# Layer 2 attention of a four-layer graph network: half of the middle graphs form their exponentials as [column, row], with squares on ScalarE

## The chip, the cores and the metric

The kernel runs on one core of a Trainium2 chip. The metric is the device time of one execution in microseconds (us), the median of three runs. PE is TensorE, PEld its weight load, DVE is VectorE, ACT is ScalarE, POOL is GpSimd and SP is SyncE.

## What is computed

32 graphs of 512 nodes with 128 features (x is 32 x 512 x 128, f32) share one adjacency matrix of 512 x 512. Four layers run one after the other, each as x = x + layer(relu(layernorm(x))). Cut to what matters here:

```
layer 0: h = x @ Wo; e[k] from pairs of u1 = h@a1, u2 = h@a2 (leaky, 0.1), masked by adj
         softmax over axis 1;  out = att @ h + x @ Ws
layer 1: h = x @ Wp + bp; scores[i,j] = leaky(src[i] + dst[j], 0.2), masked by A
         attn = softmax(scores, axis=-1) * A;  g = relu(layernorm(attn @ h) * gg + gb)
         z = relu(layernorm(((1+eps) g + A @ g) @ W1 + b1) * mg + mb);  out = relu(z @ W2 + b2 + g)
layer 2: h = x @ W; e[i,j] = leaky(f1[i] + f2[j], 0.2), -9e15 where adj[i,j] <= 0
         out = elu(softmax(e, axis=2) @ h + bias)
layer 3: out = (A3's diagonal) * (x @ W0) + (A3 without it) @ (x @ W1) + bias
```

## The kernel before, in words

A graph lies in SBUF as `xs[:, b]`, [128 partitions, 4 chunks, 128 features]: node 128c + p is partition p of chunk c. Nothing loops on the chip: the program is written out operation by operation, for every graph and layer.

**The order.** Every operation goes through `op(engine, length, emit, reads, writes)` (L130) into the `Plan`. Each layer of each graph is one chain; chains are put in order by `order` (L1320 to L1327), with `LAGS` (a layer's delay in graphs) and `GAPS` (the time between chains), stretched by `RAMP` for the first `AHEAD` graphs. `Plan.run` (L158) is a list scheduler that works before the chip does: among the operations whose inputs are there it takes the one that could begin first by the lengths given (`SLACK` apart counts as equal, then the one with the earlier turn), and emits it. The order on each engine is thus fixed and each engine works through its queue in that order. At most `WINDOW` = 20 chains are open. Buffers come from `Room`s: eight PSUM `banks`, eight `scores` tiles of [128, 4, 128] f32, six `by_act`, five `by_dve` and so on; an operation that needs a new tile waits in the plan until its room has one free. `op.port` marks operations of DVE and POOL that the plan does not let overlap. Where PE would sit idle for over `PAUSE` in the plan, `idle_products` (L331) puts in transposes whose result nobody reads. `PREPARED` and `FILLED` give the turns of the set-up of later layers' weights and masks, which runs beside the first graphs. `EARLY` says for how many graphs layer 0 normalizes on ACT rather than POOL.

**Pieces.** `preln` (L530) normalizes a graph: `variances` (L503) takes bn_stats and bn_aggr on DVE, four of each; `inv_dev` (L518) takes the power -1/2 on POOL; the normalized `xn` is transposed on PE (`turn_op`, L416, four transposes into one bank) and passed through Relu on ACT as `hT`. `project_scored` (L586) multiplies by a weight extended by two columns, so `h` has 130 columns: 128 features, the source score (column P) and the target score (column P + 1). `repeated(col)` (L604) writes a column, broadcast over 128, through four transposes, so that a bank `prow` holds the 512 values as a row in every partition.

**Attention in layers 1 and 2** is `attend` (L610). Rows i lie on partitions: for each of the four row chunks DVE adds `prow` (target scores) to the mask `bias` and takes the row's maximum (L622); two small operations make `nmax`, the negative maximum after the leaky step (L633, L637). Then, one chunk after the other: Prelu on ACT with the source score as bias (L647), Exp on ACT with `nmax` as bias and the row's sum as accumulated output (L655), four transposes on PE (L661) into a bank, a copy out as `pT` (in layer 2 two chunks on ACT, two on DVE, L666 to L671; in layer 1 a multiplication by the adjacency on DVE, L664), and four matmuls with `pT` as the stationary operand and `h` as the moving one (L675). An f32 matmul is two MATMUL instructions in the profile, a transpose is one. Layer 2 (L942) then takes the reciprocal of the sums and one DVE multiplication `v1` (L955), adds the bias on POOL (L956) and forms the elu.

**Layer 1** after its attention: variances of `po` on DVE (L886) go with the sums into a power on POOL; later the variances of `zn` on DVE (L923) go through `inv_dev`. **Layer 0** scales `h` by two per-node factors on DVE, `hs` (L805) and `hs2` (L806), and takes a masked maximum against `biasT`, the first half of the columns of the transposed mask (L727).

The lines that follow are those of the kernel before, as in the profile.

Of the kernel before, what the change touches and what calls it, by code (L numbers as in the profile page):

```python
# [35 lines left out]
AX = mybir.AxisListType  # L36

P = 128
NEG = -9.0e15
LOWEST = -3.0e38  # L40
LN_EPS = 1e-5

# [20 lines left out]

RAMP = 4.1

PAUSE = 0.6

EARLY = 8

GAPS, LAGS = (5.3, 12.0, 6.7, 5.4), (0, 6, 12, 16)  # L70


class Room:
# [38 lines left out]
class Plan:  # L112
# [45 lines left out]
    def run(self):  # L158
# [17 lines left out]
        for _ in range(len(self.ops)):  # L176
            while oldest < len(normal) and not left[normal[oldest]]:
                oldest += 1
            best = None
            for engine, ops in ready.items():  # L180
                could = []
                for op in ops:
                    k = op.chain
                    beside = self.chains[k][1] is not None
                    if not beside and order[k] >= oldest + WINDOW:
                        continue
                    begin = max(idle[engine], op.ready)
# [24 lines left out]
            if op.engine is PE and idle[PE] and begin - idle[PE] > PAUSE:  # L212
                wanted = sum(s.tile is None and s.room is self.banks for s in op.slots)
                if sum(free <= idle[PE] for free in self.banks.free) > wanted:
                    self.idle_products(begin - idle[PE])
            ready[op.engine].remove(op)
            for s in op.slots:
                if s.tile is None:
                    s.room.free.remove(min(s.room.free))
                    s.tile = s.room.make(s.name)  # L220
            end = begin + op.length
            idle[op.engine] = end
            if op.port:
                piece = op.length / op.port
                held[op.engine] = [(begin + k * piece, begin + (k + 1) * piece - HOLD) for k in range(op.port)]
            done = end + DELAY[op.engine]
            if op.load:
                bus = max(done, bus) + op.load
                done = bus
            if op.transfers:  # L230
                lanes = lanes[op.transfers :] + [done] * op.transfers
            op.emit()
            traced = nc.cur_bb.bb.instructions
            while seen < len(traced):
                ins = traced[seen]
                seen += 1
                if ins.engine in last:
                    tc.add_manual_dep(
                        ins, last[ins.engine].name,
                        mybir.DependencyInfo(mybir.DependencyClass.NoSync, mybir.DependencyReason.DATA),  # L240
                        reason="the plan's order",
                    )
                last[ins.engine] = ins
            left[op.chain] -= 1
            for s in op.slots:
                s.users -= 1
                s.until = max(s.until, done)
# [10 lines left out]
def kernel(  # L258
# [143 lines left out]
    v_offT, v_adiag, v_adiag_rep = Value(), Value(), Value()  # L402
# [37 lines left out]
    load(lambda: wt_o.t[:, 0, :], l0_wo, [wt_o], 0.25)  # L440
    load(lambda: att, l0_att.rearrange("(t p) o -> p (t o)", p=P), [v_att])
    for ib in range(C):
        load(lambda ib=ib: bias[:, ib, :], adj[blk(ib), :], [v_adj[ib]], 1.0)
    load(lambda: wts[:, W_S, :], l0_ws, [v_wts[W_S]], 0.25)
    for b in range(1, AHEAD):
        load_x(b)
# [37 lines left out]

    def mask_first():
        for jb in range(C):
            nc.vector.tensor_scalar(biasT[:, jb, :], adjT[:, jb, 0:N2], 0.0, NEG, ALU.is_le, ALU.mult)

    op(DVE, 0.85, mask_first, v_adjT[0:H], [v_biasT], port=C)

# [24 lines left out]
        dve(1.1, emit, reads, [mv])  # L515
        return mv

    def inv_dev(mv):  # L518
        rstd = Value()

        def emit():
            ve = small("ve")
            nc.gpsimd.tensor_scalar(ve, mv.own[:, :, 1], LN_EPS, 1.0, ALU.add, ALU.mult)
            rstd.own = small("rstd")
            nc.gpsimd.tensor_tensor(rstd.own, ve, mhalf, ALU.pow)  # L525

# [160 lines left out]
    def layer0(b):  # L687
# [31 lines left out]
        for hf in range(H):  # L719

            def emit_max(hf=hf):
# [3 lines left out]
                for k in range(2):  # L725
                    jb = 2 * hf + k
                    nc.vector.tensor_tensor_reduce(  # L727
                        wide(y[hf].t)[:, k * N2 : k * N2 + N2], node[:, hf, :], biasT[:, jb, :], 1.0, LOWEST,
                        ALU.add, ALU.max, rmax.own[:, jb : jb + 1],
                    )  # L730

# [74 lines left out]
        op(DVE, 0.6, lambda: nc.vector.tensor_mul(hs2.t, h[0].t[:, :, 0:P], per_chunk(rs2.own)), [rs2, *h], [hs2], port=1)  # L806

        hi, lo = [], []
        for hf in range(H):
# [51 lines left out]
    def layer1(b):  # L861
# [18 lines left out]

        def emit_ve():
            ve.own = small("ve1")
            nc.vector.tensor_add(ve.own, q.own, mv.own[:, :, 1])
# [39 lines left out]
        rz = inv_dev(variances(lambda c: zn.t[:, c, :], [zn]))  # L923

        def emit_zn():
            for c in range(C):
# [12 lines left out]
           [res], [v_x[b]], port=1)  # L939


    def layer2(b):  # L942
        hT, _ = preln(b, POOL)
        h = project_scored(hT, w2_ext, [v_w2])
        po, ssum = attend(h, lambda: h[0].t[:, :, P], h, h, None, None)
        v1 = value(by_dve, "v1")

# [5 lines left out]

        dve(0.1, emit_rs, ssum, [rs])
        dve(0.6, lambda: nc.vector.tensor_mul(v1.t, po[0].t, per_chunk(rs.own)), [*po, rs], [v1])  # L955
        op(POOL, 1.25, lambda: nc.gpsimd.tensor_add(v1.t, v1.t, row_of(B_L2)), [v_rows], [v1], port=1)  # L956


# [36 lines left out]
    def prepare():  # L995
# [24 lines left out]
        for ib in range(C):  # L1020
            dve(0.31, lambda ib=ib: nc.vector.tensor_scalar(
                bias[:, ib, :], bias[:, ib, :], 0.0, NEG, ALU.is_le, ALU.mult), [], [v_adj[ib], v_bias], port=1)
        score_weights(lambda: wt_p.t[:, 0, :], wt_p, a1[:, 0:2], v_a1, w1_ext[:, P:P2], v_w1)
        score_weights(lambda: wt_l2.t[:, 0, :], wt_l2, a2, v_a2, w2_ext[:, P:P2], v_w2)
        copy_op(DVE, 0.15, lambda: w2_ext[:, 0:P], lambda: wt_l2.t[:, 0, :], [wt_l2], [v_w2])
# [336 lines left out]
```

## Time and profile before

| | us |
|---|---|
| median of 3 runs | 1061.43 (1060.64 to 1062.57) |
| the profiled execution, its own time | 1063.87 |
| its span | 1062.1 |
| PE busy | 1041.7 (98%), 8475 instructions |
| PEld busy | 966.0 (91%) |
| DVE busy | 868.5 (82%) |
| ACT busy | 780.5 (73%) |
| POOL busy | 776.2 (73%) |

The span goes from the first to the last instruction that the profiler recorded on the core. The busy time of an engine is the union of its instructions, so where one begins before the one ahead of it has ended, the sum of the durations is larger. On PE above all: a matmul of 128 columns has a mean duration of 275 ns, and its successor starts long before it has ended. What an instruction takes away from the others is therefore read from start to start on the timeline, not from its duration. The granted clock is that of TensorE as a share of full speed.

### The profile page before, as it was taken

How to read it: one execution, taken by the hardware profiler on the slowest of the kernel's cores; microseconds unless marked ns; L12 is line 12 of the kernel's file. 1: busy time of each engine (PE TensorE's matmuls, PEld its weight loads, DVE VectorE, ACT ScalarE, POOL GpSimd, SP SyncE). 2: the span in 40 equal slices, each digit the busy share in tenths (PEclk: the TensorE clock that was granted, in tenths of full speed). 3: DMA queues.
4: the chain of work that ended last, by engine and by line, in shares of the span. 5: the costliest groups of instructions: out<-in, count | busy, mean ns of one | idle time of the engine just before them, and what ended most of it. 6: DMA issues, size and time to landing. Idle time of an engine off the chain costs nothing.

```text
span 1062.1 us, 25166 instructions
## 1 busy us (share of the span) xinstructions
PE 1041.7 (98%) x8475; PEld 966.0 (91%) x8475; DVE 868.5 (82%) x3694; ACT 780.5 (73%) x2024; POOL 776.2 (73%) x1140
## 2 busy tenths in 40 slices
PE   7899999999999999999999999999999999999998
PEld 7789789989999999999999999999899999999997
DVE  7799999989988878888888888888888877766752
ACT  6768897789877777777877777787777777767751
POOL 4489577778787777787778778777877666576772
PEclk9899999999999999999999999999999999999999
DMA  6400000000010000000000000000000000000001
GB/s 181 96 12 2 1 2 21 2 12 11 2 31 2 21 21 21 22 21 12 2 12 11 12 12 12 11 2 11 12 11 11 11 11 11 11 22 11 22 24 37
DMA packets 56912, 20.49 MB, mean 19 GB/s; under 512 B 21584, under 2 KB 56272, under 8 KB 56784
## 3 DMA queue, kind: packets, MB, share of 16 engines
q1 hardware_dynamic: 56784, 18.90, 7.2%
q8 instruction: 67, 1.10, 0.5%
q14 instruction: 61, 0.50, 0.2%
HBM read 10.43 MB, written 8.39 MB: 18 GB/s over the span
## 4 chain that ended last, share of the span: by engine, by line
PE 88%; DVE 4%; POOL 3%; DMA 1%; SPq 1%; issue 1%; ACT 1%; POOLq 0%; DVEq 0%; ACTq 0%
PE po L675 20%; PE pt L421 16%; PE po L984 10%; PE pg L911 10%; PE proj L595 7%; PE po L837 5%; PE prow L421 3%; PE p L581 3%; PE pz L581 3%; PE px L581 3%; PE po L980 3%; PE po L842 2%; PE po L834 1%; PE po L847 1%; POOL xn L560 1%
## 5 line engine op out<-in xcount | busy, mean ns | idle before, releaser
L675 PE MATMUL po<-h,pT 128*128 128x128 f32 x2048 | 242.8, 275 | 0.8 <-DVE pT L664 0.8
L675 PEld LDWEIGHTS po<-h,pT 128*128 128x128 f32 x2048 | 236.4, 192 | 5.8 <-issue 4.1
L560 POOL TENSOR_SCALAR xn<-xs,shift,rstd 128x128 f32<-128x128 f32 x480 | 213.1, 459 | 2.8 <-DVE top L633 0.9
L655 ACT ACTIVATE y<-y,nmax 128x512 f32<-128x512 f32 x256 | 181.7, 714 | 5.3 <-DVE nmax L637 4.6
L525 POOL TENSOR_TENSOR rstd<-ve,mhalf 128x4 f32<-128x4 f32 x160 | 170.9, 1068 | 13.3
L622 DVE CUSTOM_DVE_ANT_0 y<-prow,bias 128x512 f32<-128x512 f32 x256 | 162.8, 683 | 1.6 <-PE prow L421 1.6
L984 PE MATMUL po<-h,offT 128*128 128x128 f32 x1024 | 135.4, 275 | 0.0
L911 PE MATMUL pg<-adjTe,hg 128*128 128x512 f32 x256 | 131.0, 593 | 0.0
L421 PE MATMUL pt<-ident,y 128*128 128x128 f32 x1024 | 130.2, 274 | 0.7 <-ACT hl L819 0.7
L421 PEld LDWEIGHTS pt<-ident,y 128*128 128x128 f32 x1024 | 115.1, 141 | 13.8 <-issue 8.5
L984 PEld LDWEIGHTS po<-h,offT 128*128 128x128 f32 x1024 | 124.6, 192 | 0.0
L511 DVE BATCH_NORM_STATS2 st<-xs 128x6 f32<-128x128 f32 x512 | 109.8, 277 | 7.2 <-POOL xs L962 4.5
L595 PEld LDWEIGHTS proj<-w_ext,hT 128*128 128x128 f32 x768 | 96.8, 192 | 19.0 <-issue 9.6
L595 PE MATMUL proj<-w_ext,hT 128*128 128x130 f32 x768 | 102.9, 277 | 1.4 <-ACT hT L570 1.3
L647 ACT ACTIVATE y<-y,src 128x512 f32<-128x512 f32 x128 | 84.6, 714 | 20.8 <-DVE rmax L622 19.6
L962 POOL TENSOR_TENSOR xs<-xs,em 128x512 f32<-128x512 f32 x32 | 42.0, 1312 | 76.8 <-DVE em L961 63.8
L956 POOL TENSOR_TENSOR v<-v,rows 128x512 f32<-128x512 f32 x32 | 40.9, 1279 | 72.4 <-DVE v L955 72.4
L570 ACT ACTIVATE hT<-pt 128x512 f32<-128x512 f32 x128 | 73.5, 589 | 25.3 <-PE pt L421 14.0
L647 ACT ACTIVATE y<-y,h 128x512 f32<-128x512 f32 x128 | 84.7, 714 | 7.9 <-DVE rmax L622 7.7
L664 DVE TENSOR_TENSOR pT<-pt,adjT 128x512 f32<-128x512 f32 x128 | 82.6, 681 | 5.7 <-PE pt L421 5.6
L421 PE MATMUL pt<-ident,xn 128*128 128x128 f32 x512 | 77.8, 274 | 1.5 <-POOL xn L560 1.3
L412 ACT COPY h<-proj 128x260 f32<-128x260 f32 x192 | 66.1, 371 | 13.4 <-PE proj L595 12.4
(204 smaller groups left out, 2302.3 us busy)
## 6 DMA issues: line engine op xcount, KB each, us to landing
xs<-in_x_dram SPq DMA_DIRECT2D x32, 256.0 KB, 4.0
out_dram<-yo SPq DMA_DIRECT2D x32, 256.0 KB, 2.3
u<-h SPq DMA_DIRECT2D x128, 0.5 KB, 1.8
bias<-in_adj_dram SPq DMA_DIRECT2D x4, 256.0 KB, 4.4
wts<-in_L_gnn_W_dram SPq DMA_DIRECT2D x3, 64.0 KB, 4.2
rows<-in_L_gnn_bias_dram SPq DMA_DIRECT2D x2, 64.0 KB, 3.7
wt_o<-L_gnn_others_weight_dram SPq DMA_DIRECT2D x1, 64.0 KB, 2.5
wts<-n_L_gnn_self_weight_dram SPq DMA_DIRECT2D x1, 64.0 KB, 4.5
```

The source lines that it names most:

```text
L421: nc.tensor.transpose(dst(k), src(k), ident)
L511: nc.vector.bn_stats(st[:, c, :], src(c))
L525: nc.gpsimd.tensor_tensor(rstd.own, ve, mhalf, ALU.pow)
L560: nc.gpsimd.tensor_scalar(xn.t[:, c, :], src[:, c, :], shift.own[:, c : c + 1], rstd.own[:, c : c + 1], ALU.add, ALU.mult,)
L581: nc.tensor.matmul(pt.t[:, c, :], lhsT=column(hT, c), rhs=w, start=True, stop=True)
L595: nc.tensor.matmul(p[:, c, :], lhsT=column(hT, 2 * k + c), rhs=w_ext, start=True, stop=True)
L622: nc.vector.tensor_tensor_reduce(wide(y[ib].t), wide(prow.t), bias[:, ib, :], 1.0, LOWEST, ALU.add, ALU.max, rmax.own[:, ib : ib + 1],)
L647: nc.scalar.activation(yw, yw, AF.Prelu, alpha=0.2, bias=src()[:, ib : ib + 1])
L655: nc.scalar.activation(yw, yw, AF.Exp, bias=nmax.own[:, ib : ib + 1], accum_out=ssum[0].own[:, ib : ib + 1])
L675: nc.tensor.matmul(po[ib].t[:, ib, :], lhsT=pT.t[:, jb, :], rhs=h[0].t[:, jb, 0:P], start=(jb == 0), stop=(jb == C - 1),)
L911: nc.tensor.matmul(wide(pg.t), lhsT=hg.t[:, nb, :], rhs=adjTe[:, nb, :], start=(nb == 0), stop=(nb == C - 1))
L984: nc.tensor.matmul(po[ib].t[:, ib, :], lhsT=offT[:, jb, blk(ib)], rhs=h1.t[:, jb, :], start=False, stop=(jb == C - 1),)
```

## The change

`TURNED = (3, 27, 2)` picks the graphs 3, 5, 7 ... 25. In those, layer 2's attention no longer has rows on partitions when it takes the exponentials. The row maxima are found as before, into a `junk` tile. Then `p_src` and `p_max` bring the source scores and the negative maxima into two PSUM banks as rows; `r_max` is a copy of the second in SBUF. For each chunk jb of columns, DVE adds the target score (per partition), the source scores and the transposed mask; ACT takes Prelu; DVE or POOL (in turns) adds the maxima; ACT takes Exp. The result is already [column, row], and is the stationary operand of the matmuls with no transpose and no copy. The sums of the rows come from a column of ones, which is written over the source scores in `h`, so the moving operand has 129 columns. Each two chunks of rows share a bank, and are divided by their sums on DVE.

In the same graphs, the two variances of layer 1 (of `po` and `zn`) are taken on ACT as squares with an accumulated sum, and `hs2` of layer 0 is formed on ACT. `biasT` now holds all 512 columns, in bf16, and NEG is -2^53 for it. `shift`, `mv` and `rstd` get a pool with 14 buffers (8 before). The lengths and turns that the plan uses are changed.

```diff
-NEG = -9.0e15
+NEG = -(2.0**53)
+PAIRED = 1.4
-STRETCH = 3.7
-PREPARED, FILLED = (35.0, 1.2), (109.0, 1.5)
-RAMP = 4.1
+STRETCH = 3.4
+PREPARED, FILLED = (43.0, 1.2), (106.0, 1.9)
+RAMP = 3.4
-EARLY = 8
-GAPS, LAGS = (5.3, 12.0, 6.7, 5.4), (0, 6, 12, 16)
+EARLY = 10
+GAPS, LAGS = (5.0, 11.3, 6.3, 5.1), (0, 5, 11, 15)
+TURNED = (3, 27, 2)
+def is_turned(b):
+    return TURNED[0] <= b < TURNED[1] and b % TURNED[2] != 0
...
-            done = end + DELAY[op.engine]
+            done = end + (PAIRED if op.transfers > 1 else DELAY[op.engine])
...
+    sm_norm = ctx.enter_context(tc.tile_pool(name="sm_norm", bufs=14))
     def small(name, shape=(P, C)):
-        return sm.tile(list(shape), F32, name=name, tag=name)
+        pool = sm_norm if name in ("shift", "mv", "rstd") else sm
+        return pool.tile(list(shape), F32, name=name, tag=name)
...
-    biasT = const("biasT", (P, C, N2))
+    biasT = const("biasT", (P, C, N), BF16)
...
-        load(lambda: xs[:, b], x[b].rearrange("(c p) f -> p c f", p=P), [v_x[b]], 1.0)
+        load(lambda: xs[:, b], x[b].rearrange("(c p) f -> p c f", p=P), [v_x[b]], 1.35)
...
+    def squares(src, reads):
+        sq = Value()
+        def emit():
+            sq.own = small("sq")
+            for c in range(C):
+                nc.scalar.activation(sq_out, src(c), AF.Square, accum_out=sq.own[:, c : c + 1])
+        op(ACT, 1.55, emit, reads, [sq])
+        return sq
...
-        op(SP, 1.8, emit_pair, h, [u], transfers=4)
+        op(SP, 2.6, emit_pair, h, [u], transfers=4)
...
+        def emit_hs2():
+            for c in range(C):
+                nc.scalar.mul(hs2.t[:, c, :], h[0].t[:, c, 0:P], rs2.own[:, c : c + 1])
+        if is_turned(b):
+            op(ACT, 1.17, emit_hs2, [rs2, *h], [hs2])
+        else:
+            op(DVE, 0.6, lambda: nc.vector.tensor_mul(hs2.t, h[0].t[:, :, 0:P], per_chunk(rs2.own)), [rs2, *h], [hs2], port=1)
...
-        mv = variances(lambda c: po[0].t[:, c, :], po)
+        mv = (squares if is_turned(b) else variances)(lambda c: po[0].t[:, c, :], po)
...
+        if is_turned(b):
+            rz = inv_dev(squares(lambda c: zn.t[:, c, :], [zn]), lambda sq: sq.own, 1.0 / P)
+        else:
+            rz = inv_dev(variances(lambda c: zn.t[:, c, :], [zn]))
...
+    def weighed_turned(h):
+        prow = repeated(lambda k: h[0].t[:, k, P + 1 : P2], h)
+        junk = parts(scores, "junk", C)
...
+                nc.vector.tensor_tensor_reduce(
+                    wide(junk[ib].t), wide(prow.t), bias[:, ib, :], 1.0, LOWEST, ALU.add, ALU.max,
+                    rmax.own[:, ib : ib + 1],
+                )
...
+        p_src = repeated(lambda k: h[0].t[:, k, P : P + 1], h)
+        p_max = repeated(lambda k: nmax.own[:, k : k + 1], [nmax])
+        r_max = value(by_act, "r_max")
+        copy_op(ACT, 0.49, lambda: wide(r_max.t), lambda: wide(p_max.t), [p_max], [r_max])
+        y = [value(scores, "y") for _ in range(C)]
+        for jb in range(C):
+            op(DVE, 0.67, lambda jb=jb: nc.vector.scalar_tensor_tensor(
+                wide(y[jb].t), wide(p_src.t), h[0].t[:, jb, P + 1 : P2], biasT[:, jb, :], ALU.add, ALU.add),
+               [p_src, v_biasT, v_biasT2, *h], [y[jb]])
+            op(ACT, 0.61, lambda jb=jb: nc.scalar.activation(wide(y[jb].t), wide(y[jb].t), AF.Prelu, alpha=0.2), [], [y[jb]])
+            if jb % 2:
+                op(DVE, 0.61, lambda jb=jb: nc.vector.tensor_add(
+                    wide(y[jb].t), wide(y[jb].t), wide(p_max.t)), [p_max], [y[jb]])
+            else:
+                op(POOL, 1.25, lambda jb=jb: nc.gpsimd.tensor_add(
+                    wide(y[jb].t), wide(y[jb].t), wide(r_max.t)), [r_max], [y[jb]], port=1)
+            op(ACT, 0.61, lambda jb=jb: nc.scalar.activation(wide(y[jb].t), wide(y[jb].t), AF.Exp), [], [y[jb]])
+        ones = Value(h[0].slot)
+        op(POOL, 0.15, lambda: nc.gpsimd.memset(h[0].t[:, :, P : P + 1], 1.0), [neg, p_src], [*h, ones])
+        po = [value(banks, "po") for _ in range(H)]
...
+                    nc.tensor.matmul(
+                        sums(ib // 2)[:, ib % 2, 0 : P + 1], lhsT=y[jb].t[:, ib, :], rhs=h[0].t[:, jb, 0 : P + 1],
+                        start=(jb == 0), stop=(jb == C - 1),
+                    )
+            op(PE, 0.9, emit_po, [*y, ones], [po[ib // 2]])
...
+            dve(0.1, emit_rs, [po[k], *rs[0:k]], [rs[k]])
+            dve(0.35, lambda k=k: nc.vector.tensor_mul(
+                v1.t[:, 2 * k : 2 * k + 2, :], sums(k)[:, :, 0:P],
+                rs[0].own[:, 2 * k : 2 * k + 2].rearrange("p (c o) -> p c o", o=1).to_broadcast([P, 2, P]),
+            ), [po[k], rs[k]], [v1])
+        return v1
...
+        v1 = (weighed_turned if is_turned(b) else weighed)(h)
...
+        for jb in range(C):
+            dve(0.2, lambda jb=jb: nc.vector.tensor_scalar(
+                biasT[:, jb, N2:], adjT[:, jb, N2:], 0.0, NEG, ALU.is_le, ALU.mult), v_adjT, [v_biasT2], port=1)
```

More of the change, by code (lines that the diff above doesn't have):

```diff
@@ L401 @@
     v_bias, v_w1, v_w2, v_wz, v_row_p, v_row_1, v_score_p, v_adjTe, v_rows, v_mlp = (Value() for _ in range(10))
-    v_offT, v_adiag, v_adiag_rep = Value(), Value(), Value()
+    v_offT, v_adiag, v_adiag_rep, v_biasT2 = (Value() for _ in range(4))
     def load(dst, src, writes, size=0.0):
@@ L486, in mask_first @@
         for jb in range(C):
-            nc.vector.tensor_scalar(biasT[:, jb, :], adjT[:, jb, 0:N2], 0.0, NEG, ALU.is_le, ALU.mult)
+            nc.vector.tensor_scalar(biasT[:, jb, 0:N2], adjT[:, jb, 0:N2], 0.0, NEG, ALU.is_le, ALU.mult)
     op(DVE, 0.85, mask_first, v_adjT[0:H], [v_biasT], port=C)
@@ L516, in variances, with inv_dev @@
         return mv
-    def inv_dev(mv):
+    sq_out = const("sq_out", (P, P))
+    def squares(src, reads):
[6 more added lines that the diff above has]
+        return sq
+    def inv_dev(mv, of=lambda mv: mv.own[:, :, 1], share=1.0):
         rstd = Value()
@@ L522, in emit @@
             ve = small("ve")
-            nc.gpsimd.tensor_scalar(ve, mv.own[:, :, 1], LN_EPS, 1.0, ALU.add, ALU.mult)
+            nc.gpsimd.tensor_scalar(ve, of(mv), share, LN_EPS, ALU.mult, ALU.add)
             rstd.own = small("rstd")
@@ L882, in emit_ve @@
             ve.own = small("ve1")
-            nc.vector.tensor_add(ve.own, q.own, mv.own[:, :, 1])
+            if is_turned(b):
+                nc.vector.scalar_tensor_tensor(ve.own, mv.own, 1.0 / P, q.own, ALU.mult, ALU.add)
+            else:
+                nc.vector.tensor_add(ve.own, q.own, mv.own[:, :, 1])
         dve(0.08, emit_q, ssum, [q], port=1)
-        mv = variances(lambda c: po[0].t[:, c, :], po)
+        mv = (squares if is_turned(b) else variances)(lambda c: po[0].t[:, c, :], po)
         dve(0.08, emit_ve, [q, mv], [ve], port=1)
@@ L955, in layer2, with emit_top, emit_neg, emit_nmax @@
         dve(0.6, lambda: nc.vector.tensor_mul(v1.t, po[0].t, per_chunk(rs.own)), [*po, rs], [v1])
+        return v1
+    def weighed_turned(h):
+        prow = repeated(lambda k: h[0].t[:, k, P + 1 : P2], h)
+        junk = parts(scores, "junk", C)
+        rmax = Value()
+        top = [Value() for _ in range(C)]
+        for ib in range(C):
+            def emit_top(ib=ib):
+                if ib == 0:
+                    rmax.own = small("rmax")
+                nc.vector.tensor_tensor_reduce(
+                    wide(junk[ib].t), wide(prow.t), bias[:, ib, :], 1.0, LOWEST, ALU.add, ALU.max,
+                    rmax.own[:, ib : ib + 1],
+                )
+            op(DVE, 0.61, emit_top, [prow, v_bias], [junk[ib], top[ib]])
+        neg, nmax = Value(), Value()
+        def emit_neg():
+            neg.own = small("top")
+            nc.vector.scalar_tensor_tensor(neg.own, rmax.own, -1.0, h[0].t[:, :, P], ALU.mult, ALU.subtract)
+        def emit_nmax():
+            nmax.own = small("nmax")
+            nc.vector.scalar_tensor_tensor(nmax.own, neg.own, 0.2, neg.own, ALU.mult, ALU.min)
+        dve(0.08, emit_neg, [*top, *h], [neg], port=1)
+        dve(0.08, emit_nmax, [neg], [nmax], port=1)
+        p_src = repeated(lambda k: h[0].t[:, k, P : P + 1], h)
[11 more added lines that the diff above has]
+                    wide(y[jb].t), wide(y[jb].t), wide(p_max.t)), [p_max], [y[jb]])
+            else:
+                op(POOL, 1.25, lambda jb=jb: nc.gpsimd.tensor_add(
[4 more added lines that the diff above has]
+        po = [value(banks, "po") for _ in range(H)]
+        def sums(k):
+            return po[k].t.rearrange("p (c t) f -> p c (t f)", c=2)
+        for ib in range(C):
+            def emit_po(ib=ib):
+                for jb in range(C):
[4 more added lines that the diff above has]
+            op(PE, 0.9, emit_po, [*y, ones], [po[ib // 2]])
+        v1 = value(by_dve, "v1")
+        rs = [Value() for _ in range(H)]
+        for k in range(H):
+            def emit_rs(k=k):
+                if k == 0:
+                    rs[0].own = small("rs")
+                nc.vector.reciprocal(rs[0].own[:, 2 * k : 2 * k + 2], sums(k)[:, :, P])
+            dve(0.1, emit_rs, [po[k], *rs[0:k]], [rs[k]])
[3 more added lines that the diff above has]
+            ), [po[k], rs[k]], [v1])
+        return v1
```

15 lines of the change are left out of this document (8 added, 7 removed).

## The prediction, on record before the run

> **What bounds the kernel now.** I read the stage windows first: busy time of each engine in each stretch, with the granted clock.
>
> ```profile
> 0.00:50.00 50.00, 39.48 (x306) 36.12 (x307) 37.97 (x235) 34.71 (x106) 21.67 (x40) 0.97 0.57 142
> 50.00:100.00 50.00, 48.43 (x395) 46.29 (x394) 45.36 (x225) 37.74 (x115) 46.19 (x76) 0.96 0.07 12
> 100.00:150.00 50.00, 47.96 (x358) 42.22 (x357) 49.12 (x219) 38.54 (x107) 33.42 (x42) 1.00 0.02 2
> ...
> 200.00:300.00 100.00, 100.00 (x805) 91.58 (x805) 92.88 (x407) 84.19 (x226) 79.84 (x117) 1.00 0.03 7
> ...
> 500.00:600.00 100.00, 100.00 (x823) 92.91 (x823) 82.05 (x354) 72.64 (x190) 79.14 (x118) 1.00 0.05 12
> ```
>
> Columns after the stretch's length: PE, PEld, DVE, ACT, POOL, clock, DMA share, GB/s. From 200 us on PE is busy all the time at full clock, while DVE, ACT and POOL have 7 to 28% left. Before 150 us PE misses 14.1 us (50 - 39.48, 50 - 48.43, 50 - 47.96), and the windows of the tile "idle" add 131 filler products there (90 and 41).
>
> A busy PE need not be a full PE, so next I read the starts on PE's timeline:
>
> ```profile
> 501.82 1.91 PE L421 MATMUL pt<-ident,y 128*128 128x128 f32 x16
> 503.57 0.60 PE L421 MATMUL pt<-ident,zn 128*128 128x128 f32 x4
> 504.01 1.06 PE L595 MATMUL proj<-w_ext,hT 128*128 128x130 f32 x8
> 504.90 1.02 PE L911 MATMUL pg<-adjTe,hg 128*128 128x512 f32 x2
> ...
> 507.59 3.74 PE L675 MATMUL po<-h,pT 128*128 128x128 f32 x32
> 511.16 0.60 PE L421 MATMUL prow<-ident,h 128*128 128x128 f32 x4
> ```
>
> Start to start, 16 transposes take 1.75 us (0.109 each), 8 matmuls of 130 columns 0.89 (0.111 each), 32 of 128 columns 3.57 (507.59 to 511.16, 0.112 each); two of 512 columns take 0.86 (the next piece, not shown, starts at 505.76). An f32 matmul in the code is two of these instructions, a transpose one. Now the work of one graph, counts divided by 32: 64 transposes x 0.109 = 7.0; 176 matmul instructions of 128 or 130 columns x 0.112 = 19.7; 8 of 512 x 0.43 = 3.4; 8 of 256 x 0.14 = 1.1 (4 in 0.56 us at 506.12). Sum 31.2 us. The chain that ended last shows the same burst of 32 `po` at 507.75, 538.89, 570.13 and 601.27: a graph every 31.1 us. Work equals period, so **PE's throughput is the bound**: what leaves PE shortens the run, what comes to the others is free while they stay behind.
>
> The Trainium skill ("Trainium Kernel Development and Optimization", Performance Expectations) calls matmul busy time a bad measure and wants weight-load busy time instead. PEld's 92.9 of 100 would leave 7% of headroom and make any removed transpose worth less; the starts above show none, and I go by them.
>
> **The change part by part.** Turned are graphs 3, 5 ... 25: 12 of 32.
>
> *PE, layer 2.* Removed: the 16 transposes of `y` (half of the 1024 in the group shown further down are layer 2's, 16 a graph). Added: two more `repeated` calls (p_src, p_max), 8 transposes, same kind as `prow<-ident,h` (4 in 0.44). The 32 `po` instructions stay, with y in place of pT as the stationary operand and 129 columns for 128; the 130-column row has the same 0.111, so this costs nothing (bounds: 0, or 1/128 of 3.57 = 0.03 us a graph). Net -8 x 0.109 = -0.87 us a graph, **-10.5 us in all**.
>
> *DVE, by starts in its timeline.* A 512-wide copy, multiply or add takes 0.61, the 256-wide form 0.34, a group of four statistics plus aggregates 1.06 (0.78 + 0.28). Layer 2: two pT copies (-1.22), the one-piece v1 (-0.61), reciprocal (-0.1); four scalar_tensor_tensor (+2.44), two adds from PSUM (+1.22), two half v1 with reciprocals (+0.88): +2.6. Layer 1: two groups of statistics go to ScalarE, -2.1. Layer 0: hs2 goes, -0.61. Sum -0.1 a graph: nothing. No row has a bf16 second operand as biasT now is; bf16 outputs took 422 ns where f32 took 427 (512-wide mask rows), so I take no change; bounds 0 and half of layer 0's four 0.34.
>
> ```profile
> L421 PE MATMUL pt<-ident,y 128*128 128x128 f32 x1024 | 130.2, 274 | 0.7 <-ACT hl L819 0.7
> L560 POOL TENSOR_SCALAR xn<-xs,shift,rstd 128x128 f32<-128x128 f32 x480 | 213.1, 459 | 2.8 <-DVE top L633 0.9
> L956 POOL TENSOR_TENSOR v<-v,rows 128x512 f32<-128x512 f32 x32 | 40.9, 1279 | 72.4 <-DVE v L955 72.4
> ```
>
> *ACT.* Squares of 128 columns with a sum have no row. By starts, an exponential with its sum read takes 0.705 at 512 columns and 0.49 at 256, so 0.38 at 128 on the same line; from below, the scaled copy of 128 columns (L927) takes 0.295 (1.19 for 4); from above 0.49. I take 0.38: 8 x 0.38 = 3.1 a graph (2.4 to 3.9). hs2 as four scaled copies: +1.18. r_max +0.49, two pT copies -0.98, four exponentials without the sum read 4 x (0.61 - 0.705) = -0.4. Sum +3.4 (2.7 to 4.2).
>
> *POOL.* Two adds at 1.28 (the third row above; 1.279 is the mean of one) and a memset (0.10 to 0.31 in the rows of memsets): +2.7.
>
> *Are they still covered?* From the 500:600 row, a period of 31.15 holds DVE 25.6, ACT 22.6, POOL 24.7. One turned and one plain graph take 62.3 - 0.9 = 61.4 us of PE and then hold DVE 51.1 (83%), ACT 48.6 (79%), POOL 52.1 (85%). The 200:300 row shows PE full beside DVE at 93%, ACT at 84% and POOL at 80%. POOL at 85% is the only load that this run does not show beside a full PE. If the cover went, the costs above would be paid: +3.4 a graph on ACT, +2.7 on POOL, 12 times.
>
> The Trainium skill ("ScalarE: Activation LUTs", Rules for kernel authors) sends multiplications to VectorE rather than ScalarE. The trace agrees on the price: 1.18 against 0.61 for the same tile, 0.57 dearer, 6.8 us over 12 graphs. By the rule that would be a loss; while PE is the bound it is none.
>
> *The wait that is new.* In layer 2 today each row of y goes its own way to its `po`. A turned `po` needs all four y, each through four engines' steps: 0.61 DVE, 0.61 ACT, 0.61 DVE or 1.28 POOL, 0.61 ACT, at least 3.1 us by the POOL way. p_src and p_max hold two PSUM banks through it, and y and junk take five of the eight `scores` slots, not four. A waiting `po` blocks PE's queue: every projection and transpose of other graphs behind it waits too. But the order is laid out per operation with lengths 0.61, 1.25, 1.17 and 1.55, which are the slots that I read, and up to 20 chains are open, so work of other graphs should stand in front of it. I price this wait at 0; bounds 0 and the whole 3.1 us a turned graph.
>
> *The beginning.* Of its first 150 us PE loses 14.1 us idle and 131 x 0.109 = 14.3 in filler: 28 us. From 50 to 150 us DVE is busy 94.5 of 100, so DVE sets the pace there. By 150 us layer 0 has scored 11 graphs (the windows of L727: 32, 32 and 24 instructions, 8 a graph), four of them turned: -4 x 0.61. Layer 1 has reached the statistics of graph 3: -1.06. The second half of biasT adds four tensor_scalar of 256 columns, 4 x 0.25. Net **-2 us**. The new GAPS, LAGS, RAMP, EARLY, PREPARED, FILLED, STRETCH, PAIRED and load lengths only reorder. In the middle there is no idle time for a new order to win; at the beginning it can win or lose some of the 28 us. I take 0, bounds -9 and +9 (a third of it either way); the last 100 us hold only 6 us of idle time and filler.
>
> *The rest.* NEG's value, biasT's type, the arithmetic of `inv_dev` and `ve`: same instructions. sm_norm with 14 buffers frees waits such as ACT's shift for xn (9.6 us), on an engine with cover: 0. SP keeps its transfers.
>
> **Sum.** -10.5 - 2 = -12.5. The profiled execution took 1063.9 (span 1062.1, 1.8 around it), so 1051.4 like for like; the median shown is 1061.43, 2.4 lower, so **1049**.
>
> **The rivals.**
> 1. *The saving is eaten.* PE again waits 0.4 to 0.9 us a turned graph at the new `po`, or a worse order at the beginning costs 8. For: four hand-overs where there were two, and the held banks. Against: idle time before L675 is now 0.8 us over 2048 instructions. 1057 to 1063. Chance 0.13.
> 2. *Slower: the y chain is exposed.* One mechanism, at the turned `po`: it comes before its fourth y, because banks or slots are held. Paid whole, 12 x (3.1 - 0.87) = +27: 1088. It decides from 0.87 us a graph, 28% of the chain. For: POOL, at 85%, sits in the chain, and its queue holds 1.7 us normalizations (L560, four together). Against: the 200:300 row. A second table load for Square would feed the same wait: the trace has one ACT_TABLE_LOAD (1.28 us); two for each of 24 groups would put 62 us on ACT. Chance 0.13.
> 3. *It gains more*: a third of the beginning's loss also goes, below 1040. Chance 0.02.
>
> **How the numbers follow.** The forecast, 1040 to 1057, has 0.72. A measurement here can tell about 0.2% from no change, so "same" is 1059.3 to 1063.6. Rival 1 lies half in it: same 0.06; faster 0.72 + 0.07 + 0.02 = 0.81; slower 0.13. The range 1040 to 1061 holds the forecast and most of rival 1, some 0.83.
>
> **What would show it.** Right: `pt<-ident,y` falls from 1024 to 832, `prow` and its two new kin rise by 96; in the middle PE is still at 100 of 100 and two graphs take 61.4 us; `po` bursts of 129 columns still start 0.112 apart; ACT rises by about 40 us, POOL by 32, DVE stays. Wrong: idle time before the turned `po` with DVE, ACT or POOL as releaser, filler products after 150 us, a second table load, or a POOL or DVE row that lengthens because the two hold each other up.

## The result, and the profile after

| | us |
|---|---|
| before, median of 9 runs | 1062.33 (1060.64 to 1063.18) |
| after, median of 9 runs | 1065.49 (1062.15 to 1070.87) |
| ratio, 95% interval | 1.0035 [1.0018, 1.0052] |
| after, the profiled execution / its span | 1064.53 / 1062.7 |

The change makes the kernel slightly slower, where 1049 was forecast, and its times spread over 8.7 us, those of before over 2.5. The stage windows of the kernel after (columns as in the prediction):

```profile
0.00:50.00 50.00, 42.58 (x352) 39.87 (x354) 40.55 (x253) 35.41 (x106) 24.63 (x46) 1.00 0.55 139
50.00:100.00 50.00, 44.52 (x346) 41.37 (x347) 45.30 (x223) 41.22 (x127) 40.98 (x68) 0.93 0.06 10
100.00:150.00 50.00, 49.72 (x368) 43.26 (x368) 45.92 (x199) 44.36 (x132) 31.18 (x39) 1.00 0.04 7
...
200.00:300.00 100.00, 99.16 (x787) 89.59 (x786) 91.61 (x370) 91.08 (x261) 81.83 (x117) 1.00 0.04 10
...
500.00:600.00 100.00, 99.84 (x815) 92.05 (x814) 88.77 (x337) 78.85 (x223) 81.50 (x118) 1.00 0.04 10
```

The middle is no longer full, and PE runs fewer instructions there in the same time (815 for 823). The stretch from 150 to 950 us, after and then before:

```profile
150.00:950.00 800.00, 793.40 (x6375) 725.25 (x6375) 703.94 (x2688) 630.59 (x1705) 643.12 (x918) 1.00 0.05 12
```
```profile
150.00:950.00 800.00, 799.98 (x6512) 739.24 (x6511) 672.84 (x2817) 609.47 (x1568) 607.60 (x885) 1.00 0.05 12
```

Busy time hides part of it, since a matmul's record goes on while its successor is late. So I also added up, from start to start over that stretch, what exceeds the usual distance of the same kind of instruction. I call this **PE's waiting**: 0.9 us before, 17.4 us after. It belongs to the one execution that was profiled, and depends by 1 to 2 us on what is taken as usual. The removed work itself is gone. The groups of PE after:

```profile
L434 PE MATMUL pt<-ident,y 128*128 128x128 f32 x832 | 106.4, 274 | 1.5 <-ACT y L682 0.7 <-DVE ltn L781 0.3 <-DVE pT L691 0.2
L1055 PE MATMUL po<-h,y 128*128 128x129 f32 x384 | 47.1, 274 | 0.0
L434 PE MATMUL prow<-ident,h 128*128 128x128 f32 x304 | 43.7, 273 | 0.0
L434 PE MATMUL prow<-ident,nmax 128*128 128x128 f32 x48 | 7.3, 275 | 1.2 <-DVE nmax L1022 1.2
```

192 transposes of y less, 48 + 48 of the new rows more, 96 x 0.109 = 10.5 us. The turned `po` (L1055) has no idle time before it; in front of the turned graphs' `p_max` rows (`prow<-ident,nmax`) PE stands 1.2 us in all.

**Where one stall comes from.** DVE, POOL, ACT and PE on the timeline after, one fence each:

```profile
402.96 3.96 DVE L764 TENSOR_TENSOR lt<-u 128x2 f32<-128x2 f32 x1 [0.67 <-DMA u<-h]
406.96 0.16 DVE L769 SCALAR_TENSOR_TENSOR lt<-lt 128x4 f32<-128x4 f32 x1
```
```profile
403.07 1.45 POOL L854 TENSOR_TENSOR hl<-hs,hl 128x256 fp32r<-128x256 f32 x2
404.46 1.31 POOL L941 TENSOR_TENSOR hn<-hn,rows 128x512 f32<-128x512 f32 x1
405.69 1.22 POOL L905 TENSOR_TENSOR h<-h,row_p 128x512 f32<-128x512 f32 x1
```
```profile
409.68 0.37 ACT L886 COPY rest<-po 128x256 f32<-128x256 f32 x1 [3.25 <-DVE nmax L777]
...
412.63 0.58 ACT L597 ACTIVATE hT<-pt 128x512 f32<-128x512 f32 x1
```
```profile
410.14 1.95 PE L1055 MATMUL po<-h,y 128*128 128x129 f32 x16
413.26 1.16 PE L622 MATMUL proj<-w_ext,hT 128*128 128x130 f32 x8 [1.17 <-ACT hT L597]
414.26 0.27 PE L434 MATMUL pt<-ident,xn 128*128 128x128 f32 x1
414.76 1.32 PE L434 MATMUL pt<-ident,xn 128*128 128x128 f32 x3 [0.23 <-POOL xn L587]
```

An addition of two elements (lt1, two inputs in SBUF; its tile prints as `lt`) holds DVE for 3.96 us (I call this a hold-up), and ends when POOL's four instructions without a pause between them end (406.91). All that DVE has queued behind it is 4 us late; ACT stands 3.25 us; ACT's queue then holds other work before the `hT` that PE needs; PE stands. The clock pays too:

```profile
415.00:420.00 5.00, 4.80 (x15) 2.67 (x15) 3.89 (x20) 3.77 (x8) 5.00 (x11) 0.66 0.00 0
```

A granted clock of 0.66 over 5 us is 3.4 us at half speed, 1.7 us of work lost after a gap of 1.2 us. The hold-up and the gap come again at 779 us (3.95 us on L764, 1.16 us without work on PE before 789.5); there the clock stays full. In the profile of before no DVE instruction of the middle lasts longer than 1.25 us.

### The profile page after: what moved, and what is told of

The parts are those of the page before. It is cut to its first block, busy times and chain, and to the rows that moved or that the text cites. A ratio compares the mean times of both kernels' runs of the same rounds, so it can differ in the third digit from the quotient of the medians.

```text
span 1062.7 us, 25019 instructions
## 1 busy us (share of the span) xinstructions
PE 1037.7 (98%) x8371; PEld 954.3 (90%) x8372; DVE 900.7 (85%) x3568; ACT 814.8 (77%) x2210; POOL 807.5 (76%) x1168
## 4 chain that ended last, share of the span: by engine, by line
PE 75%; DVE 15%; ACT 3%; POOL 3%; DMA 2%; issue 1%; SPq 1%; DVEq 0%; POOLq 0%; ACTq 0%
PE po L702 15%; PE pt L434 12%; PE po L1109 10%; PE pg L948 8%; PE proj L622 6%; PE po L871 4%; PE prow L434 4%; DVE y L649 3%; PE po L1105 2%; PE p L608 2%; PE pz L608 2%; DVE pT L691 2%; PE px L608 2%; PE po L876 2%; DVE st L524 1%
## 5 line engine op out<-in xcount | busy, mean ns | idle before, releaser
L702 PE MATMUL po<-h,pT 128*128 128x128 f32 x1664 | 197.7, 275 | 0.3 <-DVE pT L427 0.2
L702 PEld LDWEIGHTS po<-h,pT 128*128 128x128 f32 x1664 | 191.9, 192 | 3.6 <-issue 1.9
L552 POOL TENSOR_TENSOR rstd<-ve,mhalf 128x4 f32<-128x4 f32 x160 | 175.3, 1096 | 13.3
L682 ACT ACTIVATE y<-y,nmax 128x512 f32<-128x512 f32 x208 | 147.4, 713 | 7.0 <-DVE nmax L664 7.0
L649 DVE CUSTOM_DVE_ANT_0 y<-prow,bias 128x512 f32<-128x512 f32 x208 | 133.7, 681 | 4.3 <-PE prow L434 3.8
L434 PEld LDWEIGHTS pt<-ident,y 128*128 128x128 f32 x832 | 93.4, 141 | 17.3 <-ACT y L682 10.5
L434 PE MATMUL pt<-ident,y 128*128 128x128 f32 x832 | 106.4, 274 | 1.5 <-ACT y L682 0.7
L550 POOL TENSOR_SCALAR ve<-mv 128x4 f32<-128x4 f32 x148 | 34.3, 232 | 67.8 <-DVE mv L526 35.9
L434 PE MATMUL pt<-ident,xn 128*128 128x128 f32 x512 | 82.3, 277 | 2.0 <-POOL xn L587 0.5
L434 PEld LDWEIGHTS pt<-ident,xn 128*128 128x128 f32 x512 | 61.9, 142 | 18.6 <-POOL xn L587 12.4
L871 PE MATMUL po<-hs,y 128*128 128x128 f32 x512 | 68.6, 278 | 0.1
```

The lines of the kernel that those rows point to most:

```text
L434: nc.tensor.transpose(dst(k), src(k), ident)
L649: nc.vector.tensor_tensor_reduce(wide(y[ib].t), wide(prow.t), bias[:, ib, :], 1.0, LOWEST, ALU.add, ALU.max, rmax.own[:, ib : ib + 1],)
L682: nc.scalar.activation(yw, yw, AF.Exp, bias=nmax.own[:, ib : ib + 1], accum_out=ssum[0].own[:, ib : ib + 1])
L702: nc.tensor.matmul(po[ib].t[:, ib, :], lhsT=pT.t[:, jb, :], rhs=h[0].t[:, jb, 0:P], start=(jb == 0), stop=(jb == C - 1),)
L871: nc.tensor.matmul(own, lhsT=wide(y[jb // 2].t)[:, jb % 2 * N2 + ib * P : jb % 2 * N2 + ib * P + P], rhs=hs.t[:, jb, :], start=False, stop ...
```

## The experiments

Medians in us; the kernel before lay between 1062.3 and 1063.1 in all of them. "Waiting" is PE's waiting of 150 to 950 us in the profiled execution, whose own time can lie some us from the median (e2: 1056.8 beside 1059.4; n_after_4: 1072.9 beside 1067.5). The first theories were A (the new load on POOL and DVE makes `xn` late) and B (the new order of the plan is at fault).

### The order or the load

**e1_old_order**: the plan's numbers of before.

```diff
-STRETCH = 3.4
+STRETCH = 3.7
...
-GAPS, LAGS = (5.0, 11.3, 6.3, 5.1), (0, 5, 11, 15)
+GAPS, LAGS = (5.3, 12.0, 6.7, 5.4), (0, 6, 12, 16)
```

> All of the change, but with the plan's numbers (STRETCH, PREPARED, FILLED, RAMP, EARLY, GAPS, LAGS, the transfers' lengths) of the kernel before. The changed kernel's PE starts show 17.9 us of waiting between 150 and 950 us, where the kernel before has 1.0. Theory A (the new loads on POOL and DVE, and their holding each other up, make the normalized xn late): the waiting stays, and the better beginning (some 4 us less waiting before 150 us) is lost as well: 1065 to 1071. Rival B (the new order leaves too little time between a graph's steps): the middle is full again and only PE's saving is left: 1050 to 1054.

1079.1 (ratio 1.016 [1.0144, 1.0176]), waiting 26.4: dearer than either theory said. B falls in this form: the new numbers serve the turned graphs better than the old ones. Its trace has no long hold-up on L764 (208 ns on average) and one of 4.6 us on another line (L978, at 372.75), with 2.7 us without work on PE behind it. What makes up the rest is open.

**e2_none_turned**

```diff
-TURNED = (3, 27, 2)
+TURNED = (3, 3, 2)
```

> The plan's numbers, the buffers and biasT of the change, but no graph turned and no squares or hs2 on ScalarE: PE has the work of before. Theory A: no waiting in the middle, and the beginning and the end keep their gain of some 6 us: 1055 to 1058. Rival B: the new order brings its waiting along, 17 us on top of PE's full work: 1070 to 1076.

1059.4 (0.9978 [0.9965, 0.9992]), waiting 4.8. The new order and buffers alone gain 2.9 us, and 4.8 of the 17.4 us of waiting are there with no graph turned. With 10.5 us less on PE, the turned kernel should take 1049; it takes 16.6 more.

**n_none_4** and **n_after_4**: how much is chance of the order.

```diff
-SLACK = 0.05
+SLACK = 0.04
```

> No graph turned, with SLACK 0.04 for 0.05, beside the run with 0.05 (1059.4). Where PE's work is full, PE has no waiting to gain or lose, so the order matters less: 1057 to 1062.

> The changed kernel with SLACK 0.04 for 0.05, which only changes ties in the order. It shows how much of the times is chance of the order. Theory D: another order meets other collisions of DVE and POOL, so the time moves by several us, 1056 to 1068. Rival (the turned graphs' cost is the same in any order): within 1.5 us of 1065.5.

Nothing turned: 1057.6. Turned: 1067.5, spread from 1060.2 to 1073.5, waiting 24.6. A change of ties moves a time by 2 us, so differences of that size are not read below. The second trace has six stalls of 3.7 to 4.0 us on L764; each has a PE gap of 1.2 us some ten microseconds behind it (402.9 and 413.2 the first, 788.1 and 798.1 the last).

### Which part of the change

**e3_adds_dve**: all adds of the maxima on DVE. **e4_no_adds**: none.

```diff
-            if jb % 2:
+            if True:
```

> All four adds of the maxima on DVE, from PSUM: 2.6 us a turned graph less on POOL, 1.2 more on DVE. Theory A in the form that POOL's load makes xn late: the waiting in the middle halves at least, 1052 to 1058. In the form that DVE's load (89% busy from 500 to 800 us) makes POOL late: it grows, 1068 to 1074. Rival B: as the changed kernel, 1062 to 1068.

> The adds of the maxima are left out of the turned graphs (the exponentials are taken without the subtraction of the row maximum; maxima, p_max and r_max are still formed): 2.6 us a turned graph less on POOL, 1.2 less on DVE, PE's work unchanged. Theory A: the waiting in the middle mostly goes, 1046 to 1053. Rival B: 1060 to 1067.

1058.4 (0.9960 [0.9945, 0.9975]) and 1053.5 (0.9916 [0.9902, 0.9931]); waiting 14.4 and 10.0. Taking the adds off POOL gains 7 us though DVE then carries more. Both times lie just above the ranges of theory A, and the waiting did not halve: e3 has hold-ups of its own, four of 3.7 to 4.2 us. The waits of the weight loads from 150 to 950 us (us in all, times, longest) show what the adds delay; before, after, and with the adds on DVE:

```profile
PEld pt L421 <- POOL xn L560: 0.6, 2, 0.3
```
```profile
PEld pt L434 <- POOL xn L587: 12.0, 40, 0.6
```
```profile
PEld pt L434 <- POOL xn L587: 4.4, 16, 0.3
```

PE's transposes of `xn` run at the heels of POOL's normalization, 40 times after, 2 times before. Weight loads run ahead of the matmuls, so not all of this reaches PE: by PE's starts, some 7 us of its waiting stand before transposes of `xn` after, some 2 us with the adds on DVE. The adds stand in front of the normalization in POOL's queue, as here after:

```profile
398.86 2.54 POOL L1040 TENSOR_TENSOR y<-y,r_max 128x512 f32<-128x512 f32 x2 [0.93 <-ACT r_max L425]
401.37 1.75 POOL L587 TENSOR_SCALAR xn<-xs,shift,rstd 128x128 f32<-128x128 f32 x4
```

**e5_only_layer2**, **e6_only_moves**: only the turning; only the squares and hs2 on ACT.

```diff
-        if is_turned(b):
+        if False:
             op(ACT, 1.17, emit_hs2, [rs2, *h], [hs2])
...
-        mv = (squares if is_turned(b) else variances)(lambda c: po[0].t[:, c, :], po)
+        mv = variances(lambda c: po[0].t[:, c, :], po)
```
```diff
-        v1 = (weighed_turned if is_turned(b) else weighed)(h)
+        v1 = weighed(h)
```

> Only layer 2 is turned; squares and hs2 stay on DVE as statistics and a multiplication: 2.7 us a turned graph more on DVE than in the changed kernel, 4.2 less on ACT, PE and POOL as there. Theory A (what is late is DVE and POOL, because they have too little idle time left beside the shorter PE): slower than the changed kernel, 1068 to 1076. Rival (the four squares and four scaled copies on ACT make each graph's chain longer, and that is what PE waits for): faster, 1052 to 1059.

> Squares and hs2 on ScalarE in the same 12 graphs, but layer 2 as before everywhere: PE has its full work, DVE 2.7 us a graph less, ACT 4.2 more. Theory A: PE stays full, as with no graph turned: 1057 to 1061. Rival (the work on ACT makes PE wait): 1063 or more.

1058.7 (0.9959 [0.9945, 0.9973]) and 1061.4 (1.0000 [0.9976, 1.0024]; one of its ten runs took 1074.0). DVE has 2.7 us a turned graph more to do, and the kernel is faster: A's "DVE's load" falls. The moves, meant to relieve DVE, do not help: without turned graphs they take 2.0 us (1061.4 beside 1059.4), which is within chance of the order, and leaving them out beside turned graphs gains 6.8. That this is the price of the work on ACT is not shown. e5 is another order, and no DVE instruction in its trace lasts over 2.6 us, where after has two of 4 us. With the adds on DVE, leaving the moves out gains 2.9 us (e10, below), and f7, which has the moves, and f3, which has none, differ by 0.6 us.

**e7_six_graphs**

```diff
-    return TURNED[0] <= b < TURNED[1] and b % TURNED[2] != 0
+    return TURNED[0] <= b < TURNED[1] and b % 4 == 3
```

> Every fourth graph (3, 7 ... 23) is turned, six in place of twelve: PE's work falls by 5.2 us against none turned (1059.4). Theory A, with a threshold in the idle time that is left: half the load keeps most of the saving, 1053 to 1057. If each turned graph brings its own waiting (16.6 us over 12), half of it: 1061 to 1064.

1065.1 (1.0026 [1.0017, 1.0035]), waiting 14.0: above both. There is no threshold, nor a fixed price for a graph. Neither the adds on POOL nor the hold-ups of the next section explain this run: L764 takes 184 ns on average, no DVE instruction from 150 to 950 us lasts over 1.4 us, and the weight loads wait 3.1 us for `xn`. What they wait for longest, of other engines' work, are exponentials of the old form (layer 1, and layer 2 of the graphs that are not turned); no run tried this cause:

```profile
PEld pt L434 <- ACT y L682: 11.2, 32, 1.0
```

**e8_no_memset**

```diff
-        op(POOL, 0.15, lambda: nc.gpsimd.memset(h[0].t[:, :, P : P + 1], 1.0), [neg, p_src], [*h, ones])
```

> The memset of the ones in the turned graphs is left out (the sums are then taken of the source scores): one short instruction less in POOL's queue, which stood idle for 24 us before it in the changed kernel, waiting for DVE's top and PE's p_src. Theory C (this wait holds back the xn behind it in POOL's queue): most of the waiting goes, 1052 to 1058. Theory A: the load is the same, 1062 to 1067.

1068.6 (1.0057 [1.0039, 1.0075]). C falls: without the memset the weight loads wait for `xn` as long as with it (11.8 us beside 12.0). This order has three hold-ups of 4 us on L764, where after has two.

### The collisions of DVE and POOL

**e9_one_input**: the same order, instruction for instruction, three tiny operations with one input.

```diff
-            nc.vector.tensor_add(sc.own, h[0].t[:, :, P], h[0].t[:, :, P + 1])
+            nc.vector.tensor_reduce(sc.own, h[0].t[:, :, P:P2], AX.X, ALU.add)
...
-            nc.vector.tensor_add(lt1.own, u.own[:, :, 0], u.own[:, :, 1])
+            nc.vector.tensor_reduce(lt1.own, u.own, AX.X, ALU.add)
...
-            nc.vector.scalar_tensor_tensor(lt.own, lt1_2, 0.1, lt1_2, ALU.mult, ALU.max)
+            u_2 = u.own.rearrange("p (o h) k -> p o h k", o=1).to_broadcast([P, 2, H, 2])
+            nc.vector.tensor_reduce(lt.own, u_2, AX.X, ALU.add)
```

> The changed kernel in its own order, line for line, but three tiny sums of layer 0 on DVE (sc, lt1, lt) are written as reductions over one input, where they were operations on two inputs in SBUF; lt leaves out its leaky step. In the changed kernel lt1 (two elements) took 3.96 us at 403 and at 779 us, exactly while POOL ran three adds back to back, and PE stood for 1.33 us ten microseconds later, once with half the clock for 3.4 us after it. Theory D (DVE's two-input operations are held up by POOL, and with PE's work shortened nothing is left to absorb it): the mean of L764 falls from 477 to about 170 ns, both stalls go, 1058 to 1062. Rival E (the waiting comes from the order as such, every piece of it): the time stays at 1064 to 1067.

1058.1 (0.9956 [0.9941, 0.9970]), waiting 11.2, and all five runs between 1056.5 and 1060.2. Both 4 us stalls and both PE gaps are gone, and no half clock is left in the middle. The line L764 after and here (columns: instructions, busy us, mean ns of one, idle before):

```profile
L764 DVE TENSOR_TENSOR lt<-u 128x2 f32<-128x2 f32 x32 | 15.3, 477 | 7.5 <-DMA u<-h 7.4
```
```profile
L764 DVE TENSOR_REDUCE lt<-u 128x2 f32<-128x4 f32 x32 | 4.9, 152 | 5.3 <-DMA u<-h 5.1 <-issue 0.3
```

**f6_after_4_one_input**: the same edit in the order with the six stalls.

> The order with SLACK 0.04, in which the turned kernel took 1067.5 us and L764 stood six times for 3.7 to 4.0 us, each followed some ten microseconds later by 1.3 us without work on PE; now with sc, lt1 and lt as reductions over one input (lt without its leaky step). Theory D: the six go with what hangs on them, 1054 to 1060. Rival E: 1065 to 1069.

1058.9 (0.9965 [0.9952, 0.9978]), down 8.6 us; spread 1058.2 to 1060.4; waiting 24.6 to 12.6. L764 without and with the edit:

```profile
L764 DVE TENSOR_TENSOR lt<-u 128x2 f32<-128x2 f32 x32 | 28.3, 886 | 7.7 <-DMA u<-h 7.7
```
```profile
L764 DVE TENSOR_REDUCE lt<-u 128x2 f32<-128x4 f32 x32 | 4.8, 150 | 6.6 <-DMA u<-h 6.5
```

**f1_before_one_input** and **f2_none_one_input**: the same edit where PE's work is whole.

> The kernel before with the same three operations over one input (lt without its leaky step). In its profile PE has 1.0 us of waiting from 150 to 950 us. Theory D: PE's work sets the time, collisions cost nothing there, so within 1.5 us of the kernel before. Rival F (the collisions cost the same in any of these kernels, and have nothing to do with the change): 5 us or more faster.

> The change's order with no graph turned and the three operations over one input (lt without its leaky step): beside 1059.4 without. Theory D: at most 2 us faster, 1057 to 1060. Rival F: 1052 to 1055.

1061.7 (0.9988 [0.9978, 0.9997]) and 1059.3 (beside 1059.4 without). The same edit gains 7 to 9 us in the two orders above and 0 to 1 here. That PE's full work covers the collisions here, as theory D has it, is not shown: none of the three operations lasts over 0.7 us in the kernel before, or over 1.6 us with no graph turned (e2), so there was no hold-up of 4 us to cover. The one trace of PE's whole work with a long hold-up (n_none_4) has a gap on PE eight microseconds behind it:

```profile
165.64 3.60 DVE L902 TENSOR_TENSOR src<-h,score_p 128x4 f32<-128x4 f32 x1
```
```profile
173.67 1.16 PE L871 MATMUL po<-hs,y 128*128 128x128 f32 x8 [1.18 <-DVE hs L836]
```

### The two causes together, and the version they point to

**e10_l2_adds_dve** (e3 and e5 together), **f7_adds_dve_one_input** (e3 and e9), **f5_no_adds_one_input** (e4 and e9).

> Only layer 2 turned, no squares and no hs2 on ScalarE, and all adds of the maxima on DVE: POOL and ACT carry no more than before, DVE 3.9 us a turned graph more than in the changed kernel. If the adds on POOL (7 us, by the run with the adds on DVE) and the moves to ACT (7 us, by the run with layer 2 alone) cost each for itself, 1050 to 1054; if DVE then sets the pace, 1060 or more.

> All adds of the maxima on DVE, and sc, lt1 and lt over one input (lt without its leaky step). Adds on DVE alone took 1058.4, one input alone 1058.1. Two causes beside each other: 1051 to 1054. One and the same waiting: 1056 to 1058.

> Without the adds of the maxima and with sc, lt1 and lt over one input (the exponentials without the row maximum, lt without its leaky step). PE's work is 10.5 us below that of no graph turned (1059.4), so 1049 if nothing waits. If the adds' load and the collisions are two causes beside each other: 1048 to 1051. If both removals hit the same waiting: 1053 to 1055, as without the adds alone (1053.5).

1055.5 (0.9930 [0.9915, 0.9945]), 1053.7 (0.9922 [0.9904, 0.9940]) and 1054.0 (0.9919 [0.9894, 0.9944]). e10 lies between its two ranges. The adds' place and the collisions mostly add up: 1065.5, 1058 with either mended, 1053.7 with both, 11.8 us where the two alone gave 7.1 and 7.4 (waiting 17.4, 14.4 and 11.2, 8.9). Without the adds at all, freeing the three operations gives nothing more (f5 beside e4). The six pairs side by side, from their traces and medians:

| without, with one input | sc, lt1 and lt together, ns a graph | longest of the three without, us | gain, us |
|---|---|---|---|
| before, f1 | 547, 445 | 0.7 | 1.1 |
| e2, f2 (none turned) | 948, 454 | 1.6 | 0.1 |
| e4, f5 (no adds) | 931, 456 | 2.6 | -0.5 |
| e3, f7 (adds on DVE) | 1172, 453 | 3.9 | 4.7 |
| after, e9 | 1051, 454 | 4.0 | 7.4 |
| n_after_4, f6 | 1349, 448 | 4.0 | 8.6 |

The gain does not follow the time that DVE is spared, nor whether graphs are turned: e4 has twelve turned graphs and spares DVE 15 us in all, for nothing. It comes where single hold-ups last about 4 us.

**f3_best** computes everything: e10, with sc and lt1 as reductions, and on ACT:

```diff
-            nc.vector.scalar_tensor_tensor(lt.own, lt1_2, 0.1, lt1_2, ALU.mult, ALU.max)
+            nc.scalar.activation(lt.own, lt1_2, AF.Prelu, alpha=0.1)
...
-            nc.vector.tensor_add(src.own, h[0].t[:, :, P], score_p.to_broadcast([P, C]))
+            nc.scalar.activation(src.own, h[0].t[:, :, P], AF.Identity, bias=score_p)
```

> A kernel that computes all: only layer 2 turned, all adds of the maxima on DVE, sc and lt1 as reductions over one input, lt by a Prelu and src by an Identity with a bias, both on ACT, so that none of the four can collide with POOL. Beside 1055.5 for the same without the last three. Theory D: 1050 to 1055. Rival E: 1055 to 1058.

1054.4 (0.9924 [0.9907, 0.9942]): faster than both kernels, 8.4 us below before. It is no better than e10 by more than chance of the order.

## Why the prediction was wrong

- **What bounds the kernel**: right. In the profile of before PE has 0.9 us of waiting in 800, and with no graph turned, sparing DVE 16 us in all gains nothing (f2 beside e2).
- **PE, -10.5**: right, by the counts above; and sixteen `po` of 129 columns start within 1.79 us, 0.112 each, where PE does not wait.
- **ACT +3.4, POOL +2.7 a graph**: ACT's busy time rose by 34.3 us (2.9), POOL's by 31.3 (2.6). A square with its sum takes 0.38 to 0.44 on the timeline (0.38 was taken), and there is no second table load.
- **DVE, "nothing"**: the work may be, the time is not: busy 868.5 to 900.7. Three tiny lines last longer: L764 went from 172 to 477 ns, the source score of layer 1 from 173 to 349, sc from 185 to 310; 32 x 0.61 = 19 us. With sc, lt1 and lt freed in the same order, DVE is busy 885.9 (e9). On L764 this belongs to the order more than to the turned graphs: with none turned it takes 514 ns (e2).
- **"Are they still covered?"**: the step that failed. It compared mean busy shares, 83%, 79% and 85%, with PE's period, and concluded that what comes to the others is free. Each engine works in order, so what PE waits for is not the share but the moment. POOL's adds made `xn` late (12.0 us of waits, 4.4 without them on POOL; 7.1 us of time), and DVE was held 4 us at a time (7.4 us of time, in the same order of instructions). Mending both gives back 11.8 of the 16.6 us. That PE's own work, the thing shortened, had covered such delays before is argued, not shown: before has no such hold-up. The 200:300 row, PE full beside DVE at 93%, was one stretch of one order.
- **The new wait, priced at 0**: right for the mechanism named. Nothing waits before L1055; the 1088 rival did not happen. The stalls are at `xn` and `hT`, and 1.2 us at the turned graphs' own `p_max` rows.
- **The beginning, -2**: right in size, by luck. Before 150 us PE now misses 13.2 us (14.1) and runs 112 filler products (131), some 3 us less. But with no graph turned, where none of the counted pieces leaves DVE, it misses 12.5 and runs 109 (e2): the gain is the new order's, which the sum took at 0. The terms themselves make -2.5, not -2, and the last 100 us hold 6 us of idle time and 2 of filler, not 6 of both.
- **"In the middle there is no idle time for a new order to win"**: true, but a new order could lose there, and the text gave this no price. "The saving is eaten" had 0.13 and ended at 1063 (its own terms, 12 times 0.4 to 0.9 us or 8 us on top of 1049, give 1054 to 1060); it was eaten with 6.1 us on top (1065.5 beside 1059.4).

The Trainium skill has the rule that bears on this ("SBUF — State Buffer", Who interferes with whom): DVE and GpSimd share a pair of ports as an exclusive lock, an instruction of DVE with two inputs in SBUF contends with GpSimd's reads, and `tensor_reduce` on trn2 never does. The runs agree: 477 ns against 152 for the same sum. The prediction named such a hold-up as a sign of being wrong, and gave it no price.

Open: the 5 us between the best kernels (1054) and 1049; the 1079 of the old order; why six graphs cost as much as twelve; and what the moves to ACT cost by themselves.

## What to carry to other kernels

When the bound engine's work is cut, price the others by their longest hold-ups and by what stands in front of the needed instruction in each queue, not by their busy shares: 10.5 us saved on PE came back as 16.6 us, most of it PE's waiting (17.4 us in the middle, where 4.8 stand with no graph turned). Two-input operations on tiles of a few elements are worth rewriting with one input where a trace shows them held for as long as several of POOL's instructions: it gained 4.7 to 8.6 us where the longest took 3.9 to 4.0 us, and at most 1.1 us where it took 2.6 or less. And run the change with the new order alone: here that was the part that gained.

## What was not expected of the hardware

A DVE instruction with two inputs that loses to POOL need not get its turn after one of POOL's instructions: 3.96 us through four of 0.7 to 1.3 us, with two elements to add. It need not be POOL's next pause that frees it. In e3 an addition on L764 is let through while POOL goes on without a pause, from instructions with two input tiles to the normalization (`xn`), which reads one tile and two numbers a partition:

```profile
744.40 3.85 DVE L764 TENSOR_TENSOR lt<-u 128x2 f32<-128x2 f32 x1
```
```profile
747.04 1.19 POOL L905 TENSOR_TENSOR h<-h,row_p 128x512 f32<-128x512 f32 x1
748.21 0.89 POOL L587 TENSOR_SCALAR xn<-xs,shift,rstd 128x128 f32<-128x128 f32 x2
```

The two orders with such stalls on L764 also spread widely from run to run, over 8.7 and 13.3 us, and over 3.7 and 2.2 with the three operations freed. The stalls as the reason are not shown: with no graph turned the times spread over 7.0 us, and over 7.3 with the same operations freed.

And a gap of 1.2 us on PE can be enough to halve its clock for 3.4 us, but need not be. Of eleven such gaps (1.16 to 1.19 us; two after, six in n_after_4, three in e8), two were followed by a half clock; in e3 two gaps of 1.6 us were not.
